# The last eight subtiles of a first attention layer, written in a fixed order beside fourteen output products, with some work given to GpSimd

## The chip, the cores and the metric

The kernel runs on one core of one Trainium2 chip. The metric is the device time of one launch in microseconds (us), as a median over several runs. The engines named below are TensorE (PE in the profile, its weight loads PEld), VectorE (DVE), ScalarE (ACT), GpSimd (POOL) and SyncE (SP, which here only issues transfers).

## The reference

Two cross-attention layers follow each other, all in 32-bit floats. There are 4 batches of 1024 tokens, 1024 wide, and each batch has 64 context rows.

- Layer 0: queries `x @ Wq + bq`, 32 heads of width 32, keys and values of 8 groups made from the context, scores plus a mask, softmax over 64 keys, values, then `x1 = layernorm(out @ Wo + bo + x) * gamma + beta`.
- Layer 1: keys and values of 16 heads of width 64 from the layer-normed context, queries from `x1`, softmax, values, and `y = x1 + tanh(gate) * (out @ Wo1.T)`.

## The kernel before

**Tiles.** The 4096 tokens are 32 subtiles of 128 tokens, 16 pairs of 256 and, later, 8 groups of two pairs (`NQUAD`). Eight subtiles are a block (`SUB`, `NBLK` = 4).

**Seven products for eight.** Big products are made by a Strassen-Winograd scheme: a left matrix in four blocks (A11, A12, A21 stored as S3, A22) and a right one (B11, B12 stored as T1, B22, B21) give sums S1 to S4 and T1, T2, T3, N4, and seven block products, each four 128x128 by 128x512 steps (eight matmul records) into a PSUM bank. Some banks, called X and V, stay open over several products. VectorE adds a bank into the result rows.

**Layer 0.** The queries of a block are made first (`query_steps`, L532) and stored in DRAM. `mix(t, count)` (L727) then attends to subtile t while it pulls `count` steps from the generator `other_work` (L887), which for blocks 1 to 3 makes the next block's queries. Attention of one subtile is made of two halves of 16 heads (`attend0`, L610):

- `front(c)`: scores of one half by TensorE into a two-bank PSUM tile "big" (L636), and a VectorE pass that adds the mask and writes the half to SBUF (L640). The queries of a subtile come by a 512 KB load (L603).
- `largest(e)`: VectorE maximum (L647), then VectorE subtracts it (L650). `alone` keeps some heads out of this: ScalarE then takes the exponential of these head by head with the maximum as bias (L654). For the last eight subtiles it is 4 heads of the first half.
- `exps` on ScalarE (L662), `total(e)`: VectorE sum (L667) and reciprocal (L668), `divide(e)`: VectorE product (L671). Each of these VectorE passes covers 128x1024 numbers.
- `flip(c)`: eight TensorE transposes (L408) and a ScalarE copy to SBUF (for the last eight subtiles two copies of a bank each, L411); `values`: 16 small matmuls (L715), ScalarE copies (L399, or L401 in one piece) and a store of the subtile's output to DRAM (L721).

**The last eight subtiles** (24 to 31, L951 to 955) have no next block to prepare. They run beside 32 steps of `folded_queries` (L848), which multiply layer 1's query weight by its keys: four matmuls each (eight records, L858), two ScalarE copies (L864), and after every second step a 1 MB store issued by GpSimd (`ad<-a`, L870); the weights of four steps come in one 512 KB load (`turned_chunk`, L843). Eight of the 32 steps go ahead of subtile 24 (`FOLD_AHEAD`). The four sums of the right factor Wo (`right_sums`, L188) and the sums of the left factor of pair 0 (`left_out`, L425) are VectorE's. The products of pair 0 (`products`, L449) follow the folded steps (L459): four within subtile 31's `mix`, two around the last flips, one after.

**The order up to here** is a scheduler's: it places the recorded instructions on each engine. From L1047 on (`manual_schedule`) they stand as written. There a small planner takes over: `job(at, end, ...)` puts VectorE, ScalarE, GpSimd and SP work into time slots beside a list of TensorE steps, with due times; it fixes an order, and the hardware still waits by semaphores.

**From L1047 on.** Pair 1's products run as phase ("o", 0) by the list `PAIR`, with four steps F. F is `fold` (L1428): four matmuls (eight records) of layer 1's values and output weight, two ScalarE copies, two 512 KB stores. Then come groups 1 to 7, phases ("o", k), each with two pairs P and Q, by the lists `FOLD_FIRST` (k = 1) and `FOLD`, with three F each for k = 1 to 4, and `MIX` afterwards. In these, joint products a, b, c of both pairs take the place of separate ones; GpSimd makes their sums (L1150, L1154, L1542) and adds the bias `bo` to rows (L990). `close_row` (L1461) normalizes a finished row tile and stores it as `x1`. Layer 1 follows.

**Room.** The pool `weights` has seven 8 KB tiles of the tag "wb": the folded results, the weight chunks, the first rows. `foldpool` has one tile for both kT and vT. `wx` are four single PSUM banks, `big` two double ones. SP issues all loads in order; a load whose room is not free holds those behind it.

## Time and profile before

| what | value |
|---|---|
| median of 3 runs | 1864.75 us (1863.9 to 1869.64) |
| the profiled execution's own time | 1861.73 us |
| its span, first to last instruction | 1859.5 us |
| mean granted TensorE clock | 0.992 of full |
| DRAM to SBUF and back | 355.03 MB, 190 GB/s over the span |
| values of subtile 22 done, on TensorE | 584.6 us |
| scores of subtile 24 start | 593.0 us |
| first product of pair 0 / of pair 1 / of group 1 | 683.3 / 716.4 / 748.8 us |

The stage that the change touches lies from about 585 to 749 us, followed by groups 1 to 4 up to about 961 us. In a timeline line of the profile the first number is the start, the second the time from the first instruction's start to the last one's end, then engine, line, operation, tiles and count; the brackets give the idle time ahead of it and what ended it. A line of a table by stretches gives each engine's busy time in that stretch, with the number of instructions, then the granted clock, the share of the transfer engines that was busy (it can pass 1 a little) and the bytes moved per second.

### The profile page before, as it was taken

How to read it: one execution, taken by the hardware profiler on the slowest of the kernel's cores; microseconds unless marked ns; L12 is line 12 of the kernel's file. 1: busy time of each engine (PE TensorE's matmuls, PEld its weight loads, DVE VectorE, ACT ScalarE, POOL GpSimd, SP SyncE). 2: the span in 40 equal slices, each digit the busy share in tenths (PEclk: the TensorE clock that was granted, in tenths of full speed). 3: DMA queues.
4: the chain of work that ended last, by engine and by line, in shares of the span. 5: the costliest groups of instructions: out<-in, count | busy, mean ns of one | idle time of the engine just before them, and what ended most of it. 6: DMA issues, size and time to landing. Idle time of an engine off the chain costs nothing.

```text
span 1859.5 us, 22201 instructions
## 1 busy us (share of the span) xinstructions
PE 1809.2 (97%) x6856; PEld 1025.0 (55%) x6856; DVE 1368.5 (74%) x1800; ACT 745.0 (40%) x2960; POOL 736.9 (40%) x726
## 2 busy tenths in 40 slices
PE   8999999999999889999999999999999999999998
PEld 7744444444445654455556545656655665566555
DVE  3525589789879995566677887887779777977773
ACT  1111475675635763333322221571607160716150
POOL 0006011111100102833434427658556755675563
PEclk9999999999999899999999999999999999999999
DMA  8996499998786985744567454564378338833741
GB/s 282 182 224 195 131 257 269 258 266 246 225 241 210 324 298 201 270 159 153 181 210 203 147 137 101 165 175 136 114 193 215 113 114 195 213 114 114 181 158 69
DMA packets 228597, 355.03 MB, mean 191 GB/s; under 512 B 29568, under 2 KB 150784, under 8 KB 225280
## 3 DMA queue, kind: packets, MB, share of 16 engines
q1 hardware_dynamic: 175376, 259.23, 49.6%
q0 software_dynamic: 15216, 60.83, 10.8%
q10 hardware_dynamic: 37888, 33.56, 6.1%
q8 instruction: 55, 0.90, 0.2%
q14 instruction: 62, 0.51, 0.1%
HBM read 209.63 MB, written 143.92 MB: 190 GB/s over the span
## 4 chain that ended last, share of the span: by engine, by line
PE 70%; DMA 12%; DVE 10%; ACT 4%; issue 3%; POOL 1%; SPq 1%; DVEq 0%; ACTq 0%; POOLq 0%
PE wx L1085 29%; PE joint L1162 19%; PE wx L532 11%; PE big L636 2%; DMA b_B<-bd 2%; PE wx L380 2%; PE big L380 1%; DMA xq<-in_x_dram 1%; PE big L1438 1%; ACT s L654 1%; DVE s L640 1%; PE big L715 1%; DVE s L671 1%; DMA a_B<-ad 1%; DMA q<-qTd 1%
## 5 line engine op out<-in xcount | busy, mean ns | idle before, releaser
L1296 ACT ACTIVATE s<-s,mx 128x64 f32<-128x64 f32 x512 | 169.9, 334 | 387.3 <-DVE mx L1294 376.5
L654 ACT ACTIVATE s<-s,mx 128x64 f32<-128x64 f32 x488 | 162.7, 336 | 77.1 <-DVE mx L647 74.0
L1096 DVE TENSOR_TENSOR r<-wx,r 128x512 f32<-128x512 f32 x133 | 88.8, 684 | 88.2 <-PE wx L1085 79.5
L990 POOL TENSOR_TENSOR r<-r,bo 128x512 f32<-128x512 f32 x60 | 82.6, 1401 | 147.6 <-DMA r<-in_x_dram 112.3
L532 PE MATMUL wx<-xT,wq_S 128*128 128x512 f32 x256 | 116.6, 599 | 0.8 <-ACT z L543 0.8
L532 PE MATMUL wx<-xB,wq_A 128*128 128x512 f32 x256 | 113.8, 595 | 0.0
L1306 ACT ACTIVATE s<-s,sm 128x64 f32<-128x64 f32 x448 | 108.4, 334 | 12.8 <-DVE sm L1304 12.8
L695 POOL DMA_DIRECT2D pq<-p x76 | 41.5, 553 | 165.1 <-DVE pT L420 66.3
L1469 ACT ACTIVATE junk<-r 128x1024 uint8<-128x1024 f32 x32 | 33.8, 1056 | 167.2 <-DVE r L1176 143.4
L636 PEld LDWEIGHTS big<-kv,q 64*128 64x128 f32 x1024 | 70.0, 193 | 49.4 <-issue 45.3
L640 DVE TENSOR_TENSOR s<-big,m 128x1024 f32<-128x1024 f32 x64 | 77.5, 1216 | 25.0 <-PE big L636 23.6
L1296 ACT ACTIVATION_READ_ACCUMULATOR s<-s,mx 128x1 f32 x512 | 95.9, 187 | 0.0
L814 POOL DMA_DIRECT2D wq1T<-wq1c x64 | 34.9, 552 | 149.3 <-DVE wq1c L420 147.3
L654 ACT ACTIVATION_READ_ACCUMULATOR s<-s,mx 128x1 f32 x488 | 91.9, 188 | 0.0
L1172 DVE TENSOR_TENSOR r<-joint,r 128x256 f32<-128x256 f32 x126 | 52.8, 421 | 41.4 <-PE joint L1162 40.1
L636 PE MATMUL big<-kv,q 64*128 64x128 f32 x1024 | 81.6, 290 | 1.4 <-DMA q<-qTd 1.4
L1176 DVE TENSOR_TENSOR r<-joint,r 128x512 f32<-128x512 f32 x84 | 57.4, 687 | 33.9 <-PE joint L1162 33.7
L532 PEld LDWEIGHTS wx<-xB,wq_A 128*128 128x128 f32 x256 | 48.2, 190 | 58.6 <-issue 57.1
L532 PEld LDWEIGHTS wx<-xT,wq_S 128*128 128x128 f32 x256 | 47.5, 190 | 58.8 <-issue 55.0
L671 DVE TENSOR_TENSOR s<-s,sm 128x1024 f32<-128x1024 f32 x64 | 77.1, 1216 | 1.0
L647 DVE TENSOR_REDUCE mx<-s 128x16 f32<-128x1024 f32 x64 | 75.2, 1212 | 0.9
L870 POOL DMA_DIRECT2D ad<-a x16 | 12.1, 753 | 149.4 <-ACT a L864 149.4
(331 smaller groups left out, 4364.3 us busy)
## 6 DMA issues: line engine op xcount, KB each, us to landing
p<-s POOLq DMA_DIRECT2D x19, 1024.0 KB, 7.7
pq<-p POOLq DMA_DIRECT2D x76, 256.0 KB, 5.9
xq<-in_x_dram SPq DMA_DIRECT2D x64, 256.0 KB, 9.9
q<-qTd SPq DMA_DIRECT2D x32, 512.0 KB, 7.5
oTd<-oT ACTq DMA_DIRECT2D x32, 512.0 KB, 7.2
ad<-a POOLq DMA_DIRECT2D x16, 1024.0 KB, 9.3
r<-in_x_dram SPq DMA_DIRECT2D x32, 512.0 KB, 5.6
bd<-b ACTq DMA_DIRECT2D x32, 512.0 KB, 7.9
```

Source lines behind the costliest of these rows:

```text
L532: nc.tensor.matmul(bank, w_q[a][:, k, sub_ap(i)], rows[b][:, k, :], start=first and k == 0, stop=last and k == HK - 1, skip_group_check=True,)
L636: nc.tensor.matmul(ps[:, at : at + P], q[on, c * 4 + g, :], k0bd[on, b, c, :], start=True, stop=True,)
L640: nc.vector.tensor_tensor(quarters[:, :, c * 8 : (c + 1) * 8], ps.rearrange("p (k a l) -> p a k l", a=NQ, l=Q), mask.rearrange("p e (h l) ...
L647: nc.vector.tensor_reduce(mx[:, e], heads[:, e], AX.XY, ALU.max, negate=True)
L654: nc.scalar.activation(heads[:, e, k], heads[:, e, k], AF.Exp, bias=mx[:, e, k : k + 1], accum_out=sm[:, e, k : k + 1],)
L671: nc.vector.tensor_tensor(heads[:, e], heads[:, e], wide(sm[:, e]), ALU.mult)
L990: on.tensor_tensor(columns(row, h), columns(row, h), bo_sb[h], ALU.add)
L1085: nc.tensor.matmul(banks[key, i], left_at(left[i][s], k), w[m][:, k, :], start=first and k == 0, stop=last and k == HK - 1, skip_group_che ...
L1096: nc.vector.tensor_tensor(at, bank, at, ALU.add)
L1162: nc.tensor.matmul(ps[key], block(a)[:, k, :], (rb | sums[j] if sums else rb)[b][:, k, :], start=first and k == 0, stop=last and k == 1, s ...
L1296: nc.scalar.activation(v[:, h], v[:, h], AF.Exp, bias=mx[:, h : h + 1], accum_out=sm[:, h : h + 1])
L1306: nc.scalar.activation(v[:, h], v[:, h], AF.Copy, scale=sm[:, h : h + 1])
```

## The change

- Subtiles 24 to 31 are no longer given to the scheduler. `manual_schedule` opens ahead of them, and the new `last_mix` writes their order by hand, with a table `PLAN`: for each subtile the number of folded steps, the number of products, and a piece of work (load a pair, make its left sums, add a bias).
- The products of both first pairs are made by `products`: 11 inside the eight subtiles, one after the last folded step, one between the last flips and values, one behind them. The phase ("o", 0) with its list `PAIR` is gone. Its four F go elsewhere: two to the head of `FOLD_FIRST`, and one more to each `FOLD`.
- GpSimd takes the second division of each of the eight subtiles, all four sums of Wo in eight halves (`split_sums`), the left sums of pair 1, and the bias of the first four row tiles (`add_bias_early`, with a bias tile of its own).
- For these subtiles ScalarE copies a double bank at once (L415, L401), and no head has its exponential alone.
- Loads: the four blocks of Wo are asked for ahead of the folded steps, the rows and outputs of pair 0 in subtile 24 and of pair 1 in subtile 27; vT, two chunks of Wo1 and half of group 1's left factor after the last folded step. Six weight chunks and the bias have a pool of three tiles of their own.
- The row tiles 0 to 3 are closed in group 1, and group 1's rows and joint sums get other due times.

```diff
         order = [
             ("X", "A11", "B11", True, False, 0, 0),
+            ("W", "A12", "B21", True, True, 0, 0),
             ("X", "S2", "T2", False, False, 1, 0),
...
-            ("W", "A12", "B21", True, True, 0, 0),
         ]
...
-        alone = BY_HEAD if by_turning(t) else (4, 0) if t >= NSUB - SUB else (0, 0)
+        alone = BY_HEAD if by_turning(t) else (0, 0)
...
         def divide(e):
-            nc.vector.tensor_tensor(heads[:, e], heads[:, e], wide(sm[:, e]), ALU.mult)
+            on = nc.gpsimd if e and t >= NSUB - SUB else nc.vector
+            on.tensor_tensor(heads[:, e], heads[:, e], wide(sm[:, e]), ALU.mult)
...
-            turn(s[:, c * 1024 : (c + 1) * 1024], pT, t >= NSUB - SUB)
+            turn(s[:, c * 1024 : (c + 1) * 1024], pT)
...
+            whole = by_turning(t) or t >= NSUB - SUB - 1
+            ps = big() if whole else [wx(), wx()]
...
+    def split_sums(r):
+        return [
+            lambda o=o, x=x, y=y, k=k: nc.gpsimd.tensor_tensor(r[o][:, k], r[x][:, k], r[y][:, k], ALU.subtract)
+            for o, x, y in (("T1", "T1", "B11"), ("T2", "B22", "T1"), ("T3", "T2", "B11"), ("N4", "B21", "T2"))
+            for k in (slice(0, 2), slice(2, 4))
+        ]
...
+        bias.append(turnedpool.tile([P, H], F32, tag="wq", name="bias_0"))
+        wT, ahead = turned_chunk(0), []
+        nc.sync.dma_start(out=bias[0], in_=bo0.partition_broadcast(P))
         w_o, w_o_loads = right_loads(wo0, "wa", "wo0", "heads")
+        run(w_o_loads)
...
+            for n, step in enumerate(folded_queries(kT, wT, k)):
                 step()
+                for _ in range({11: 1, 12: 1, 14: 2}.get(4 * k + n, 4 * k + n > 14 and len(sums) > 0)):
+                    sums.pop(0)()
                 yield
...
+        vT = foldpool.tile([P, KC, B * S], F32, tag="kvT", name="vT")
+        nc.sync.dma_start(out=vT, in_=vTd)
+        for k in range(2):
+            chunks[k] = chunk(wo1, k, "wo1")
...
+    def last_mix(t, folds, n, then):
+        front, largest, exps, total, divide = attend0(t)
+        front(0)
+        front(1)
+        if t + 1 < NSUB:
+            load_queries(t + 1)
+        next(work)
+        then()
+        largest(0)
+        exps[0]()
+        if n:
+            ready.pop(0)()
+        if t - 2 in turned:
+            turned.pop(t - 2)[1]()
+        turned[t - 1][0](0)
+        largest(1)
+        exps[1]()
+        next(work)
+        total(0)
+        divide(0)
+        turned[t - 1][0](1)
+        total(1)
+        divide(1)
+        for _ in range(2, folds):
+            next(work)
+        turned[t] = outputs0(t)
+        if n > 1:
+            ready.pop(0)()
...
+    PLAN = (
+        (5, 0, first_pair), (2, 2, first_left), (3, 1, lambda: None), (2, 2, second_pair),
+        (3, 1, lambda: None), (2, 2, second_left), (3, 1, lambda: None), (4, 2, lambda: add_bias_early(first_pair_rows[1])),
+    )
+    for i, (folds, n, then) in enumerate(PLAN):
+        last_mix(last + i, folds, n, then)
+        if makes:
+            makes.pop()()
+    next(work)
+    ready.pop(0)()
+    turned.pop(NSUB - 2)[1]()
     flip, values = turned.pop(NSUB - 1)
-    first.pop(0)()
     flip(0)
     flip(1)
-    first.pop(0)()
+    ready.pop(0)()
     values()
...
-    FOLD_FIRST = ("P1 P7 F P6 " + LEAVES).split()
-    FOLD = ("P1 | P6 | P7 F " + LEAVES).split()
-    PAIR = "P1 P7 F P6 P2 F P5 P4 F P3 F".split()
+    FOLD_FIRST = (
+        "F F P1 Q1 P6 F P7 P5 cS1 cS2 cS3 cS4 aS1 aS2 F Q7 c2 c1 Q6 c6 aS3 a2 c7 aS4 Q5 " + END
+    ).split()
+    FOLD = ("P1 | P6 | F P7 F " + LEAVES).split()
...
-    go(phase(("o", 0), [ahead_a], w_o, [second_rows], joint=False), PAIR)
+    bo_sb = both_halves(bo0, "bo")
     for i in range(2):
-        turn("o", 1, i, 3.0 * i, 12.0, (28.0, 44.0)[i], lands=8.0, room=lambda: True)
+        turn("o", 1, i, -1.0, 4.0 + 12.0 * i, (6.0, 22.0)[i], lands=6.0 + 10.0 * i, room=lambda: True)
+    output_rows(1, -1.0, 28.0)
```

## The prediction

> **What bounds the kernel now.** I read the page first, then the stage by stretches, then the timelines of TensorE and VectorE, the chain of waits and the transfers.
>
> ```profile
> span 1859.5 us, 22201 instructions
> ...
> PE 1809.2 (97%) x6856; PEld 1025.0 (55%) x6856; DVE 1368.5 (74%) x1800; ACT 745.0 (40%) x2960; POOL 736.9 (40%) x726
> ```
>
> TensorE sets the end: 97% busy. But the share is an average, and busy is a modelled figure. By stretches of 20 us, the last eight subtiles stand out:
>
> ```profile
> 600.00:620.00 20.00, 15.52 (x113) 10.87 (x112) 15.41 (x17) 15.73 (x38) 1.51 (x2) 0.83 1.05 362
> 620.00:640.00 20.00, 17.44 (x166) 13.03 (x164) 19.38 (x22) 15.49 (x41) 3.01 (x4) 1.00 0.91 293
> 640.00:660.00 20.00, 18.19 (x162) 13.29 (x162) 19.27 (x27) 15.15 (x33) 1.51 (x2) 0.91 1.06 362
> 660.00:680.00 20.00, 14.65 (x118) 11.41 (x118) 17.71 (x18) 14.73 (x38) 2.26 (x3) 0.91 0.88 298
> ```
>
> TensorE (first busy figure) has gaps and a lowered clock, VectorE (third) is full, GpSimd (fifth) nearly empty, the transfer engines (last two) saturated in two of the four. After 720 us TensorE is at 20 of 20 in most stretches, so only this stage can give much. VectorE's period, from one subtile's scores to the next's:
>
> ```profile
> 622.89 2.35 DVE L640 TENSOR_TENSOR s<-big,m 128x1024 f32<-128x1024 f32 x2
> 625.27 2.35 DVE L647 TENSOR_REDUCE mx<-s 128x16 f32<-128x1024 f32 x2
> 627.54 2.08 DVE L650 TENSOR_TENSOR s<-s,mx 128x768 f32<-128x768 f32 x2
> 630.17 2.16 DVE L667 TENSOR_REDUCE sm<-s 128x12 f32<-128x768 f32 x2 [0.55 <-ACT s L662]
> 632.25 0.37 DVE L668 RECIPROCAL sm<-sm 128x16 f32<-128x16 f32 x2
> 632.54 2.35 DVE L671 TENSOR_TENSOR s<-s,sm 128x1024 f32<-128x1024 f32 x2
> 634.81 2.35 DVE L640 TENSOR_TENSOR s<-big,m 128x1024 f32<-128x1024 f32 x2
> ```
>
> It is 11.9 us, nearly all work. TensorE's work beside it is less, and after each gap of some 2 us it runs slowly:
>
> ```profile
> 603.21 2.81 PE L715 MATMUL wx<-pT,kv 64*32 64x512 f32 x16 [2.05 <-ACT pT L415]
> 607.39 2.08 PE L636 MATMUL big<-kv,q 64*128 64x128 f32 x16 [1.36 <-DMA q<-qTd]
> 609.23 1.94 PE L858 MATMUL wx<-kT,wq1T 64*128 64x256 f32 x8
> 610.93 1.13 PE L636 MATMUL big<-kv,q 64*128 64x128 f32 x16
> ```
>
> The same 16 score matmuls take 2.08 us and, 3.5 us later, 1.13.
>
> **How much is there.** From 584.6 (values of subtile 22 done) to 748.8 (first product of group 1) are 164.2 us. TensorE's work in it, from dense rows: 32 folded steps at 1.03 (61 records in 7.82 us, eight a step) 33.0; 16 score halves at 1.05, 16.8; nine pairs of flips at 1.97, 17.7; nine values at 1.05, 9.5; 14 products at 3.44 (starts 716.38 and 719.82) 48.2; four F at 1.92 (starts 723.34 and 725.26) 7.7. Sum 132.9, so 31.3 us are gaps and slow running. The change keeps all this work and moves the four F behind the first product of group 1 or into groups 1 to 4, where TensorE has no gap to hide them: they cost 7.7 there as here. So compare one point, T, the end of the 14th product: before it is 748.8 - 7.7 = 741.1, and it can't be below 584.6 + 125.2 = 709.8. Gain = 741.1 - T, plus what changes in group 1.
>
> **The new cycle.** VectorE a subtile: four times 2.35 (scores, maxima, subtraction, sums, now all of 1024), one division 1.18, reciprocals 0.37: 10.9. Dropping `alone` adds 0.46 of that (2.08 and 2.16 become 2.35) and takes four head-by-head exponentials (1.35 from 614.61 to 615.96) off ScalarE. A product's addition is 0.69.
> - Subtile with one product, three folded steps: VectorE's first addition stands between the two subtractions and waits for scores 1.05, folded step 1.03, product 3.44, 0.2 latency: 5.7 after the period's start. After it 0.6, then maximum, subtraction, sums, division (five passes of 1.18) and reciprocals 0.4: 12.6. TensorE's work, 2.1 + 3.1 + 3.44 + 1.05 + 1.97 = 11.7, lies inside.
> - Two products, two steps: TensorE 2.1 + 2.06 + 6.88 + 1.05 + 1.97 = 14.1, VectorE inside.
> - Subtile 25 also has pair 0's left sums on VectorE, 2.7 (653.61 to 656.3): 12.6 + 0.6 + 2.7 = 15.9.
>
> Subtile 24's scores still wait for their query load (VectorE idles 1.01 ahead of 594.46), so three right sums of 2.28, 2.23 and 2.28 taken from VectorE at 581 to 593 give nothing by themselves. Start of 24: 594.5; of 25: 605.4; then 15.9, 12.6, 14.1, 12.6, 14.1, 12.6 to subtile 31 at 687.3; its TensorE work with four steps, 16.1 less the 1.05 already done; then three products, two values, one pair of flips, 14.4. T = 716.8, if nothing is late.
>
> **What can be late.**
> - *Transfers.* The second load of the burst at subtile 24 took 18 us:
>
> ```profile
> 589.12 18.14 DMA q<-qTd
> ```
>
> It competes with four 1 MB stores issued from 588.7 to 594.6. The change queues 1 MB more ahead of subtile 25's queries on SP (bias, one chunk earlier) and 2 MB (rows and outputs of pair 0) behind them, ahead of subtile 25's first product. At the 410 GB/s seen there 1 MB is 2.6 us: queries at about 610 to 611 instead of 607.3, when VectorE could start at 605.4: 6 late. Pair 0's 2 MB need 5.1 more and share with stores: 617 to 619, when TensorE wants them at 614: 4 late, and the product then starts at a lowered clock. Bounds 0 (burst over sooner) and 14; I take 10. From subtile 26 on a subtile moves some 2.6 MB in 13 us, 200 GB/s, and there is slack.
> - *GpSimd's passes.* No row shows its division of 128x1024. Nearest are its 128x512 sums, 1.28 alone and 1.83 crowded: 2.5 to 3.7. It starts when VectorE goes on to the next scores and is wanted 8 us into the next period: nothing, unless GpSimd is held by a store's wait. Taking the division off VectorE is in the 10.9.
> - *VectorE beside GpSimd.* In group 1 the two disturb each other:
>
> ```profile
> 754.23 1.28 POOL L1542 TENSOR_TENSOR sums_a<-wo_B 128x512 f32<-128x512 f32 x1
> 759.61 1.71 POOL L1542 TENSOR_TENSOR sums_a<-sums_a,wo_B 128x512 f32<-128x512 f32 x1
> ```
> ```profile
> 760.12 3.42 DVE L1490 SCALAR_TENSOR_TENSOR r<-r,norm,beta 128x512 f32<-128x512 f32 x2
> 804.50 1.41 DVE L1490 SCALAR_TENSOR_TENSOR r<-r,norm,beta 128x512 f32<-128x512 f32 x2
> ```
>
> Alone 1.28 and 0.70 (1.41 for two), side by side 1.71 each. So a VectorE pass of 1024 with two SBUF inputs (subtraction, division) may lose 2.0 beside GpSimd. The eight halves of Wo's sums lie in subtiles 24 to 27, three such passes each: bounds 0 and 9 x 2.0 = 18. By the written order the sums meet one subtraction in subtile 26 and little in 25, where VectorE waits for loads: I take 2.
> - *Start of group 1.* SP's second bias load of the planner reuses room of the last output store; before it stood 23 us for that (issue 694.76 to 717.7) and came 3.5 after the store's issue. After, the store is issued 1.9 ahead of T, so the load comes at T + 1.6, behind it the row tile (median landing 5.6) and two GpSimd bias passes: ready at T + 11. The third product of group 1 needs sums that stand behind that addition on VectorE: it starts at T + 13 instead of T + 10.8 (F F 3.9, two products 6.9). Group 1 before loses 2.81 at 764.26 and 2.0 by a product of 5.40 after it; I set one against the other: 0, bounds -5 and +5.
> - *A fourth F a group* needs a free "wb" tile; ScalarE waited 7.3 for such stores in all before. Bounds 0 and 4, I take 0.
> - Whole-bank copies: 0.99 for two of 0.58, off the path: 0, either way.
>
> **The sum.** T = 716.8 + 10 + 2 = 728.8; gain 741.1 - 728.8 = 12.3. The profiled execution is 1861.7 (span 1859.5 and 2.2 around it): 1849.4. It lies 3.0 below the median of the three runs, so 1852.4 for a median: 1852.
>
> *A rule that speaks against the change.* The Trainium skill, "SBUF — State Buffer", section "SBUF: two separate sides", says that a VectorE pass with two SBUF inputs and a GpSimd pass that reads SBUF exclude each other for a whole instruction. The rows above agree in kind (1.71 is about one pass behind the other, not a small tax). Taken at its worst, each of the nine passes waits out a GpSimd half of 2.6, some 23 us (an estimate from that page and the 1.28 row), and the gain would be gone.
>
> **The rivals.**
> 1. *Loads on time.* For it: from subtile 26 there is slack, and the burst's length is seen once only. Against: 408 to 414 GB/s from 596 to 608. T = 718.8, gain 22: 1842.
> 2. *TensorE closes up.* Waits overlap, VectorE's addition costs less than reckoned; T comes within 4 of its floor, 709.8, group 1 loses its stall: gain 30, 1835.
> 3. *Nothing to speak of.* The load burst at its upper bound 14 and the collisions at 6 to 8: gain 12.3 - 4 - 5 = 3: 1861. This also holds the case that the fixed order only moves the gaps.
> 4. *Slower.* Group 1's start, starved of loads: vT shares one tile with kT, so its load waits for the last folded step, and SP holds all of group 1's loads behind it; 7 MB then stand in one queue from about T - 17. If the first biased row is ready not at T + 11 but past T + 29, as when it lands as late as the 18 us load and the bias waits behind it, the stall eats the 12.3 and 5.6 more; at T + 35 the time is 1864.8 + 10 = 1875. Against: transfers are light there (some 60 to 260 GB/s before), and the needed row is seventh or so in the queue.
>
> **How the numbers follow.** Forecast (gain 6 to 18) 0.43; rival 1 0.26; rival 2 0.07; rival 3 0.13; rival 4 0.11. A measurement of this kernel can tell about 0.3%, 5.6 us, from no change: faster 0.76, same 0.13, slower 0.11. The range leaves out the lowest of rival 2 and most of rival 4 and takes in the bounds of loads and collisions: 1835 to 1866.
>
> **What would show it.** Right: subtile periods (L640) of about 12.6 and 14.1 in turn from 26 on; GpSimd's first division beginning as the next scores' pass does; a first gap ahead of subtile 25's scores or its first product, ended by a load of q or o; the 14th product ending near 729; four F in each of groups 1 to 4, TensorE without gaps there. Wrong: no such gap (rival 1); periods of 15 us and more, with VectorE's L650 or L672 stretched to over 2 us (collisions); a long stop ahead of group 1's third product, ended by a load or a bias (rival 4). A mistake in the cycle itself would show as TensorE idle in the two-product subtiles.

## The result, and the profile after

The changed kernel takes **1889.70 us** (median of 4 runs, 1889.32 to 1897.76), the kernel before 1864.33 (4 runs, 1862.05 to 1869.64): a ratio of 1.0142, with the interval 1.0108 to 1.0177. It is slower by some 25 us, where 12 were to be gained. The profiled execution took 1889.41 us; its span is 28.1 us longer than before's.

The head of the page of the changed kernel:

```profile
span 1887.6 us, 22128 instructions
...
PE 1813.6 (96%) x6856; PEld 1020.2 (54%) x6856; DVE 1379.3 (73%) x1777; ACT 734.9 (39%) x2871; POOL 789.2 (42%) x753
```

TensorE's busy time is 4 us more, the span 28: the rest is idle. VectorE has fewer instructions than before and more busy time, so some of them got longer. The stage in stretches of 20 us (columns as before: TensorE, its weight loads, VectorE, ScalarE, GpSimd, clock, share of the transfers, GB/s):

```profile
600.00:620.00 20.00, 11.58 (x73) 8.31 (x72) 10.94 (x7) 6.18 (x12) 13.33 (x8) 0.72 1.05 404
620.00:640.00 20.00, 20.00 (x131) 10.49 (x132) 17.26 (x21) 7.00 (x9) 6.85 (x5) 0.94 0.47 143
...
680.00:700.00 20.00, 15.00 (x94) 8.99 (x94) 19.79 (x14) 6.26 (x8) 13.68 (x13) 0.85 0.46 149
...
800.00:820.00 20.00, 18.16 (x72) 12.96 (x70) 14.74 (x22) 5.39 (x11) 19.86 (x16) 1.00 0.40 155
```

Two things differ from before. In the first line everything waits: TensorE 11.6, VectorE 10.9, with the transfers full. In the line from 680, VectorE is "busy" for 19.79 us with 14 instructions, of which none takes more than 1.23 alone (17 together at most); that is where GpSimd, too, is busiest in the stage. Behind the stage, at 800, GpSimd is full.

Where nothing disturbs it, the cycle is as forecast. The timeline of subtile 28 on VectorE:

```profile
665.27 2.36 DVE L640 TENSOR_TENSOR s<-big,m 128x1024 f32<-128x1024 f32 x2 [0.20 <-issue]
...
668.91 1.22 DVE L650 TENSOR_TENSOR s<-s,mx 128x1024 f32<-128x1024 f32 x1
...
677.91 2.36 DVE L640 TENSOR_TENSOR s<-big,m 128x1024 f32<-128x1024 f32 x2
```

The period is 12.64 us (12.6 was forecast), the subtraction 1.22. One subtile later, in the timeline of VectorE and GpSimd:

```profile
680.65 0.80 POOL L873 DMA_DIRECT2D ad<-a  x1 [0.82 <-ACT a L867]
681.47 2.42 POOL L435 TENSOR_TENSOR S<-o 128x256 f32<-128x256 f32 x2
681.55 1.75 DVE L650 TENSOR_TENSOR s<-s,mx 128x1024 f32<-128x1024 f32 x1
683.86 1.41 POOL L435 TENSOR_TENSOR S<-S,o 128x256 f32<-128x256 f32 x2
685.09 8.75 DVE L650 TENSOR_TENSOR s<-s,mx 128x1024 f32<-128x1024 f32 x1
685.23 1.26 POOL L443 TENSOR_TENSOR o<-o 128x512 f32<-128x512 f32 x1
686.46 1.40 POOL L435 TENSOR_TENSOR S<-o,S 128x256 f32<-128x256 f32 x2
687.83 4.92 POOL L973 TENSOR_TENSOR r<-r,bias 128x512 f32<-128x512 f32 x4
```

The second subtraction starts at 685.09 and ends at 693.84, 1.09 us after GpSimd's last pass (692.75). VectorE does not lose one pass of GpSimd; it waits out the whole run and then does its own work. Such a wait is called a lock below. Five subtractions of the stage end like that: 6.05 at 615.17, 3.03 at 638.73, 3.43 at 654.01, 8.75 at 685.09 and 5.10 at 715.41 (with the 1.75 of 681.55, an excess of 20.8 us over 1.22 each). Each ends 1.09 us after the end of a run of GpSimd passes, and in front of each of the five runs stands a store issued by GpSimd, like the one at 680.65. The three long ones (6.05, 8.75 and 5.10) wait for two, eight and four passes; those of 3.03 and 3.43 begin when a single pass of 2.3 us is left, so they would also fit a wait for one pass. How a lock reaches TensorE, in the timeline of ScalarE and TensorE at the place just shown:

```profile
693.88 1.06 ACT L662 ACTIVATE s<-s 128x1024 f32<-128x1024 f32 x1 [6.92 <-DVE s L650]
695.79 1.01 ACT L415 COPY pT<-big 128x1024 f32<-128x1024 f32 x1
696.86 2.08 PE L636 MATMUL big<-kv,q 64*128 64x128 f32 x16 [5.00 <-ACT pT L415]
```

ScalarE's exponentials wait 6.92 us for the subtraction, the copy behind them is late, and TensorE waits 5.00 for the bank that the copy frees. The load burst is there too, on TensorE:

```profile
608.76 3.66 PE L636 MATMUL big<-kv,q 64*128 64x128 f32 x32 [4.45 <-DMA q<-qTd]
616.98 6.36 PE L461 MATMUL wx<-wo_B,o 128*128 128x512 f32 x8 [3.70 <-DMA o<-oTd]
764.64 5.40 PE L1163 MATMUL wx<-wo_T,S_o 128*128 128x512 f32 x8 [4.09 <-DVE S_o L1113]
```

Subtile 25's queries stop it for 4.45, pair 0's outputs for 3.70, and the product after the second gap runs slowly (6.36 for some 3.6). The third line is group 1's third product.

**Where the 28 us are.** Compare T, the end of the 14th product (before 741.1, forecast 728.8, after 749.0), and the first products of the groups behind it. All four F of pair 1 have moved, so their number in each stretch has to be taken into account.

| stretch | before | after | difference with equal F |
|---|---|---|---|
| up to T | 741.1 | 749.0 | +7.9 |
| T to group 2's start | 61.5 with 7 F | 65.2 with 4 F | +3.7 and 3 F (5.8): +9.5 |
| groups 2 to 4 | 158.3 with 9 F | 172.5 with 12 F | +14.2 less 3 F (5.8): +8.4 |
| the rest | | | +2.3 |

T is counted from an execution's first instruction, and the executions are not equally far when the stage begins: the values of subtile 22 are done at 584.6 in the profile of the kernel before, at 581.2 in the change's. From there to T it is 156.5 before and 167.8 after, 11.3 us more; the prediction's sum gave 144.2 (728.8 - 584.6).

The stage's periods, from one subtile's scores to the next's, are 20.4, 23.6, 15.3, 14.9, 12.6, 20.6 and 13.3, then 37.2 to T; without lateness 10.9, 15.9, 12.6, 14.1, 12.6, 14.1, 12.6 and 29.5 were reckoned. The long ones are 24 (loads), 25 (loads and a lock together), 29 and the end.

### The profile page after: what moved, and what is told of

Same layout as the page of the kernel before. It is cut to its first block, busy times and chain, and to the rows that moved or that the text cites. A ratio compares the mean times of both kernels' runs of the same rounds, so it can differ in the third digit from the quotient of the medians.

```text
span 1887.6 us, 22128 instructions
## 1 busy us (share of the span) xinstructions
PE 1813.6 (96%) x6856; PEld 1020.2 (54%) x6856; DVE 1379.3 (73%) x1777; ACT 734.9 (39%) x2871; POOL 789.2 (42%) x753
## 4 chain that ended last, share of the span: by engine, by line
PE 65%; DVE 12%; DMA 11%; ACT 5%; issue 4%; POOL 1%; SPq 1%; ACTq 0%; DVEq 0%; POOLq 0%
PE wx L1163 24%; PE joint L1240 17%; PE wx L532 13%; PE big L636 2%; PE wx L461 2%; DMA b_B<-bd 2%; PE wx L380 1%; PE big L380 1%; DMA x<-r 1%; ACT s L654 1%; DVE s L650 1%; DVE s L640 1%; DMA p<-s 1%; DMA r<-in_x_dram 1%; PE big L717 1%
## 5 line engine op out<-in xcount | busy, mean ns | idle before, releaser
L1374 ACT ACTIVATE s<-s,mx 128x64 f32<-128x64 f32 x512 | 169.9, 333 | 389.2 <-DVE mx L1372 378.2
L654 ACT ACTIVATE s<-s,mx 128x64 f32<-128x64 f32 x456 | 151.9, 336 | 68.2 <-DVE mx L647 65.3
L1174 DVE TENSOR_TENSOR r<-wx,r 128x512 f32<-128x512 f32 x126 | 83.8, 684 | 79.4 <-PE wx L1163 61.8
L1374 ACT ACTIVATION_READ_ACCUMULATOR s<-s,mx 128x1 f32 x512 | 95.6, 187 | 0.0
L654 ACT ACTIVATION_READ_ACCUMULATOR s<-s,mx 128x1 f32 x456 | 85.8, 188 | 0.0
L1176 DVE TENSOR_TENSOR s<-wx,key_bias 128x512 f32<-128x512 f32 x64 | 42.9, 683 | 37.3 <-PE wx L1163 25.3
L672 DVE TENSOR_TENSOR s<-s,sm 128x1024 f32<-128x1024 f32 x56 | 67.9, 1217 | 1.2
```

The lines of the kernel that those rows point to most:

```text
L654: nc.scalar.activation(heads[:, e, k], heads[:, e, k], AF.Exp, bias=mx[:, e, k : k + 1], accum_out=sm[:, e, k : k + 1],)
L672: on.tensor_tensor(heads[:, e], heads[:, e], wide(sm[:, e]), ALU.mult)
L1174: nc.vector.tensor_tensor(at, bank, at, ALU.add)
L1374: nc.scalar.activation(v[:, h], v[:, h], AF.Exp, bias=mx[:, h : h + 1], accum_out=sm[:, h : h + 1])
```

## The experiments

The theory after reading the two traces: the stage is lost to VectorE's subtractions that wait for runs of GpSimd passes, and behind T the work that stood beside pair 1's products now crowds groups 1 to 4. The rivals: the load burst alone makes the stage late; or group 1 is starved by its loads (rival 4 of the prediction). Each run below is the changed kernel with one edit, unless told otherwise. T and the groups are from the one profiled execution, in us. "Stage" is from the end of subtile 22's values to T: that end lies between 580.5 and 585.6 in these executions, so "stage" compares better than T. "P to P" is from group 1's first product to group 2's, with 2 F in the change, 3 before and in spread_folds, 5 in calm_front and calm_all; "2 to 4" is the sum of these groups, with 12 F in the change and 9 in three_folds, calm, calm_front, calm_all and spread_folds.

| run | median (range) | ratio to before (95%) | T | stage | P to P | 2 to 4 | group 5 |
|---|---|---|---|---|---|---|---|
| before | 1864.33 | 1 | 741.1 | 156.5 | 53.8 (3 F) | 158.3 (9 F) | 46.0 |
| the change | 1889.70 (1889.32–1897.76) | 1.0108–1.0177 | 749.0 | 167.8 | 60.8 | 172.5 | 46.0 |
| left_bias_moved | 1889.58 (1886.66–1896.21) | 1.0106–1.0162 | 745.2 | 163.0 | 63.3 | 174.1 | 46.4 |
| wo_sums_vector | 1895.97 (1894.18–1900.05) | 1.0139–1.0181 | 751.8 | 167.8 | 63.2 | 174.3 | 46.0 |
| bo_by_gpsimd | 1887.38 (1882.40–1889.48) | 1.0091–1.0136 | 748.3 | 167.3 | 57.3 | 175.0 | 46.0 |
| three_folds | 1896.29 (1891.63–1898.52) | 1.0159–1.0200 | 750.0 | 167.8 | 61.3 | 161.3 | 64.4 |
| bias_behind | 1890.05 (1887.44–1896.55) | 1.0130–1.0179 | 749.2 | 167.9 | 61.0 | 168.7 | 46.0 |
| later_products | 1902.51 (1900.59–1903.94) | 1.0200–1.0231 | 761.8 | 177.3 | 63.0 | 170.2 | 46.4 |
| calm | 1880.56 (1877.95–1885.17) | 1.0078–1.0125 | 742.6 | 160.5 | 55.5 | 159.3 | 61.4 |
| calm_front | 1883.54 (1881.12–1887.55) | 1.0082–1.0121 | 742.1 | 160.7 | 72.8 | 162.0 | 46.0 |
| lighter_burst | 1892.20 (1888.52–1895.09) | 1.0127–1.0161 | 748.9 | 166.6 | 63.6 | 174.6 | 46.0 |
| calm_all | 1873.11 (1871.08–1874.19) | 1.0027–1.0056 | 731.8 | 148.7 | 73.3 | 160.0 | 46.5 |
| stores_by_scalar | 1878.50 (1876.87–1883.41) | 1.0054–1.0101 | 735.9 | 154.4 | 61.3 | 171.0 | 46.0 |
| division_vector | 1897.23 (1892.70–1898.72) | 1.0138–1.0193 | 755.6 | 170.0 | 63.5 | 172.4 | 46.2 |
| all_four_folds | 1865.80 (1860.01–1874.40) | 0.9992–1.0024 | 729.2 | 148.7 | 55.3 | 172.5 | 46.0 |
| all_scalar_stores | 1868.53 (1861.60–1872.77) | 1.0004–1.0037 | 734.6 | 153.0 | 58.6 | 169.3 | 46.6 |
| spread_folds | 1872.36 (1869.88–1876.33) | 1.0032–1.0063 | 731.8 | 148.8 | 57.7 | 161.6 | 56.5 |

They are told in the order in which they ran.

### First: who is in VectorE's way

**left_bias_moved.** Pair 1's left sums go back to VectorE, the early bias behind the subtiles.

```diff
-        products_of(second_pair_rows, "0_1", nc.gpsimd)
-        makes.pop()()
-        add_bias_early(second_pair_rows[1])
+        products_of(second_pair_rows, "0_1", nc.vector)
...
+    add_bias_early(first_rows)
+    add_bias_early(second_rows)
     next(work)
```

> Edit to the changed kernel: pair 1's left sums go from GpSimd to VectorE, at the end of subtile 29, and the bias of the first four row tiles is added by GpSimd behind its last division instead of in subtiles 29 and 31. Theory 1 (VectorE's subtraction stands still as long as GpSimd has passes in a row): the subtraction of 8.75 us in subtile 29 and that of 5.10 in subtile 31 become 1.2 each; VectorE gets 2.7 of sums; the period of subtile 29 falls from 20.6 to about 14, the 14th product ends near 740 instead of 749.0, and the whole is 7 to 10 us shorter, about 1881. Rival (the long subtraction only covers what TensorE or a load would lose anyway): periods stay within 2 us, the time within 3 us of 1890.

The long subtractions of subtiles 29 and 31 are gone, so GpSimd's run is their cause. But T came only 3.8 earlier, to 745.2, not to about 740, and the stage is 4.8 shorter: VectorE's own sums cost 2.7 in period 29, TensorE had new gaps in period 30 (1.58 and 1.33), and the late bias held a product's addition at the end (a gap of 2.12). Groups 1 to 4 then gave it back (63.3 for 60.8 and 174.1 for 172.5), and the median did not move. The cause is right, the size of the gain was not.

**wo_sums_vector.** The four sums of Wo return to VectorE, two of them in subtile 24.

```diff
-        sums = split_sums(w_o)
+        sums = right_sums(w_o)
```

> Edit to the changed kernel: the four sums of Wo go from eight GpSimd passes in subtiles 24 to 27 to four VectorE passes, two ahead of subtile 24's scores and two behind its last sum, where VectorE stands idle for 7.7 and 9.0 us. Theory 1: the subtractions of 6.05, 3.03 and 3.43 us in subtiles 25, 26 and 27 become 1.2. Since subtile 25's first product waits for its load until 617 and ends at 623.4 whatever VectorE does, the first of these gives nothing, the other two 2 to 3 us: about 1887. Rival (the 6.05 us subtraction is what makes subtile 25 late): 6 to 8 us, about 1882. If instead the sums push subtile 24 back, the time rises by up to 4.

The long subtractions of 25 to 27 are gone. Yet subtile 26 still starts 25.0 behind 25 (612.94 to 637.89; 23.6 in the change), because the first product waits 5.55 for its load, to 620.72: the 6.05 lay beside a wait for data and cost little by itself. Two other runs say the same: in bo_by_gpsimd and three_folds, whose stage is the change's, this subtraction began just ahead of GpSimd's run and took 1.2, and subtile 25's period was 25.0 and 25.2 all the same. Subtile 29's first subtraction became one of 11.23, where the two had been 1.75 and 8.75. The stage is as long as the change's (167.8); T is later only because this execution was 2.8 later when the stage began. The median is 6.3 higher; of that the trace shows 4.2 in groups 1 to 4, and why they are longer is open.

**bo_by_gpsimd.** The planner's bias load goes to GpSimd's queue, so that SP's is free.

```diff
-    bo_sb = both_halves(bo0, "bo")
+    bo_sb = both_halves(bo0, "bo", nc.gpsimd)
```

> Edit to the changed kernel: the load of the planner's bias, for which SyncE stands still from 732.4 to 750.5 until the last output store has left, is issued by GpSimd, which is idle then; SyncE can go on to group 1's remaining left factor and rows. Theory (the held queue makes group 1's start late): the first row lands before 750 instead of 761.6, VectorE's first addition no longer waits 11.8 us for it, TensorE's gap of 4.09 at 760.6 and the slow product of 5.40 behind it go, and the whole is 5 to 7 us shorter, about 1884. Rival (the room of these rows is itself taken as long, or the biased row is late for GpSimd's sake): the gap stays within 1 us and the time within 2 us of 1890.

In the changed kernel SP stands on this load from 732.39 to 750.5, because its room comes from the last output store. The group 1 lines of the changed kernel's timeline:

```profile
732.39 18.15 SPq L1055 DMA_DIRECT2D bo<-in_bo_dram  x2
...
761.63 0.69 DVE L1174 TENSOR_TENSOR r<-wx,r 128x512 f32<-128x512 f32 x1 [11.82 <-DMA r<-in_x_dram]
```

The rows come behind it and land 12.6 after T. With the edit the gap of 4.09 and the slow product behind it are gone and P to P falls by 3.4; groups 2 to 4 give 2.5 back. The median falls by 2.3, where 5 to 7 were expected. So rival 4's mechanism exists, for 3.4 us and not for 28.

**lock_probe** leaves the whole computation out and lets VectorE and GpSimd passes run against each other.

> A kernel that leaves the whole computation out and only times VectorE and GpSimd passes side by side; its output is mostly a copy of x. GpSimd runs of eight 128x512 subtractions, 1.27 us each alone, beside VectorE passes that start 0.7 us later. Theory 1 (starvation): one 128x1024 subtraction of two SBUF inputs takes about 1.2 plus all that is left of GpSimd's run, 9 to 10 us in all. Rival (exclusion for one instruction at a time): it waits out one GpSimd pass, 1.2 + 1.3 = at most 2.5 us, and three in a row alternate with GpSimd's passes. VectorE passes with one SBUF input (maxima) or with a PSUM input keep 1.2 us in both. If nothing is stretched, the 8.75 us in the changed kernel have another cause.

Alone, a VectorE pass of 128x1024 with two SBUF inputs takes 1.22 and a GpSimd pass of 128x512 1.26. Side by side they take turns: 2.10 to 2.17 and 2.24. Maxima (one input) and a pass with an input in PSUM are not touched (1.21, 1.22). No pass waited out a run, so the mechanism that I had named, starvation by back-to-back passes alone, is not it.

### Second: behind the stage

**three_folds.** Three F a group instead of four; the freed ones fall to group 5.

```diff
-    FOLD = ("P1 | P6 | F P7 F " + LEAVES).split()
+    FOLD = ("P1 | P6 | P7 F " + LEAVES).split()
```

> Edit to the changed kernel: three F instead of four in each of groups 2 to 4, as before; the three left over go to group 5. Nothing ahead of group 2 is touched. From group 2's first product to that of group 5 the changed kernel takes 172.5 us, the kernel before 158.3; 5.8 of the difference are three F, 8.4 are gaps of TensorE that end with GpSimd's sums lS or VectorE's additions. Theory (the fourth F of a group pushes row closings, row loads and with them GpSimd's bias in front of lS): the stretch takes about 158 to 160, and with 5.8 of F in group 5 the whole is 6 to 8 us shorter than 1889.6, about 1882. Rival (these groups are late because group 1 hands them its lateness): the stretch still takes 165 or more after the 5.8 are taken off, the time stays within 3 us.

Groups 2 to 4 fall from 172.5 to 161.3: 5.8 for three F, and 5.4 of gaps that the fourth F had brought. But group 5 with three F takes 64.4, where 46.0 and 5.8 make 51.8. Its timeline:

```profile
1006.29 2.12 ACT L1519 ACTIVATE b<-big,tanh_gate 128x1024 f32<-128x1024 f32 x2 [9.04 <-DMA bd<-b]
1007.46 3.78 PE L1516 MATMUL big<-wo,vT 64*128 64x512 f32 x8 [5.38 <-ACT b L1519]
```

ScalarE waits 9.04 for a store to free its output tile, TensorE 5.38 for ScalarE, and the next F runs slowly (3.78 for 1.99). The time rose by 6.6 us, where a fall of 6 to 8 was expected. F has a price by its place.

**bias_behind.** GpSimd's bias passes get later due times in groups 3 to 5, so that joint sums come first.

```diff
-                return now + 9.0
+                return now + (14.0 if 2 < k < 6 else 9.0)
```

> Edit to the changed kernel: the planner's guess of how long a row load of groups 3 to 5 takes goes from 9 to 14 us, so that GpSimd's bias of one row, which waits about 10 us for that load, stands behind the last two of the four sums lS instead of in front of them. Four F a group stay. Theory of the order (lS behind a bias that waits for a load is what holds TensorE): the stops for lS in groups 3 and 4 (1.9, 1.3 and 0.2 us, each with some slow running after it) go, 3 to 5 us shorter, about 1885. Rival (the rows themselves are late because of the fourth F, whatever the order): the gaps move to VectorE's additions of group 4 and 5, time within 2 us of 1889.6.

Groups 2 to 4 take 168.7 instead of 172.5: in the changed kernel GpSimd stood still for a row's load (9.63 before a bias pass at 917.05) with joint sums behind it that TensorE then waited for. The order is worth 3.8 in the trace. The profiled execution was 2.0 faster, the median the same: smaller than this measurement tells.

**later_products.** Subtile 24 without loads of pair 0, everything one subtile later.

```diff
-        (5, 0, first_pair), (2, 2, first_left), (3, 1, lambda: None), (2, 2, second_pair),
+        (4, 0, lambda: None), (5, 0, first_pair), (2, 2, first_left), (2, 2, second_pair),
```

> Edit to the changed kernel: the first products move from subtile 25 to subtile 26, pair 0's loads from subtile 24 to 25, and each later subtile takes a product more instead (folded steps 4, 5, 2, 2, 3, 2, 3, 3). Theory (subtiles 24 and 25 are held by a burst of transfers: scores at 611.5 instead of 605.4, the first product at 617 for its load and 6.4 us long): subtile 25 runs without the wait for pair 0's outputs, its period falls from 23.6 to 15 or less; the product it gives up costs 3.4 later; the 14th product ends 3 to 6 us earlier, at about 744, and the time is near 1886. Rival (the burst only moves on): subtile 25's scores still start at 611, and subtile 26 waits for pair 0's outputs instead: no gain or a loss of up to 4.

Slower by 13, more than either the theory or its rival had said. Subtile 25's scores still came only at 616.7, two subtractions became 10.21 and 9.92 long, and T went to 761.8, with a stage of 177.3.

**calm** joins four edits: pair 1's sums on VectorE and the bias late, `bo` by GpSimd, three F.

> Four edits to the changed kernel together: pair 1's left sums by VectorE; the early bias by GpSimd behind its last division, pair 1's rows first; the planner's bias loaded by GpSimd; three F a group. If each of the losses stands by itself, their sum goes: 4 to 6 in the stage, 3 in group 1, 6 to 8 in groups 2 to 4: about 1873 to 1876. If groups 1 to 5 are held by a chain that does not run through TensorE's stage (rows, closings, GpSimd's sums), what is won in the stage is lost again in group 1, as in the run that moved left sums and bias: 1880 or more.

T falls by 6.4 to 742.6 (the stage by 7.3), P to P to 55.5, groups 2 to 4 to 159.3 (158.3 before), and group 5 takes 61.4, near the 64.4 of three_folds. The median falls by 9 us, to 1880.6, where 1873 to 1876 stood for losses that add up. In the trace those ahead of group 5 do add up; the 9.6 that group 5 takes beyond its three F is more than what is missing.

### Third: the burst, and why the lock is kept

**calm_front** is calm with the F of group 5 in group 1 (seven there).

```diff
-        "F F P1 Q1 P6 F P7 P5 cS1 cS2 cS3 cS4 aS1 aS2 F Q7 c2 c1 Q6 c6 aS3 a2 c7 aS4 Q5 " + END
+        "F F P1 Q1 F F P6 F P7 P5 F cS1 cS2 cS3 cS4 aS1 aS2 F Q7 c2 c1 Q6 c6 aS3 a2 c7 aS4 Q5 " + END
```

> The kernel with four edits (left sums of pair 1 by VectorE, early bias behind the last division, the planner's bias loaded by GpSimd, three F a group) with the three F that had gone to group 5 put into group 1 instead, two of them behind its first two products. There group 5 took 61.4 us, 9.6 more than 46.0 and three F. Theory (F suits a group as long as its output tile and weights come free in time; group 1 has gaps that F can fill): group 5 is back at 46, group 1 grows from 55.5 by 4 to 6, groups 2 to 4 stay near 159: 1880.6 less 9 to 11, about 1871. Rival (F's outputs wait for room wherever the fourth and further F stand): group 1 grows by 12 or more and the time stays at 1878 to 1882.

Group 5 is back at 46.0, but P to P is 72.8: TensorE waited 3.92 and 4.46 for ScalarE's output of F and 4.84 for GpSimd's joint sums. The gain of the one is the loss of the other, and about 1871 was missed by 12.

**lighter_burst.** The bias load moves out of subtile 24, and pair 0's outputs are asked for ahead of its rows.

```diff
         r = wpool.tile([P, 2, H], F32, tag="wb", name=f"r0_0_{pair}")
-        for u in range(2):
-            nc.sync.dma_start(out=r[:, u], in_=x[sub_ap(2 * pair + u), :])
         o = pool.tile([P, KC, 2 * P], F32, tag=tag, name=f"o2_{pair}")
         nc.sync.dma_start(out=o, in_=oTd[pair])
+        for u in range(2):
+            nc.sync.dma_start(out=r[:, u], in_=x[sub_ap(2 * pair + u), :])
```

> Edit to the changed kernel: the early bias is loaded in subtile 27 instead of ahead of subtile 24, and of a pair's two loads the outputs go ahead of the rows. Theory (bytes queued ahead of what subtile 25 needs make it late): 0.5 MB less is 1.3 us at 410 GB/s and the order of the pair's loads another 2.6: scores of subtile 25 start at about 610 instead of 611.5, its first product at 613 instead of 617; the first addition can still not come before 621 because VectorE's subtraction waits for GpSimd until then, so the 14th product ends 2 to 4 us earlier and the time is 1886 to 1888. Rival (the four and more stores of 1 MB own the transfer engines whatever is asked for behind them): no change within 1.5 us.

Its timeline:

```profile
609.53 2.36 DVE L640 TENSOR_TENSOR s<-big,m 128x1024 f32<-128x1024 f32 x2 [5.90 <-DMA m<-in_mask_dram]
612.85 3.67 PE L461 MATMUL wx<-wo_B,o 128*128 128x512 f32 x8 [1.32 <-DMA o<-oTd]
613.17 6.33 DVE L650 TENSOR_TENSOR s<-s,mx 128x1024 f32<-128x1024 f32 x1
```

The loads come earlier: scores at 609.5 for 611.5, the first product at 612.9 for 617.0, and at full speed. Subtile 26 is not earlier (636.0 for 635.1), and T is 748.9: a subtraction of 6.33 and a left sum of 5.63 take the place of the load. This mirrors wo_sums_vector. Two waits lie side by side in subtile 25, and to take away one of them gains nothing: the median, 1892.2, is no better than the change's.

**calm_all** is calm_front with the lighter burst and the sums of Wo earlier.

```diff
-                for _ in range({11: 1, 12: 1, 14: 2}.get(4 * k + n, 4 * k + n > 14 and len(sums) > 0)):
+                for _ in range({7: 2, 11: 4, 17: 1, 18: 1}.get(4 * k + n, 0)):
```

> All edits together: those of the kernel with seven F in group 1, the lighter burst, and the first six of Wo's eight half sums moved ahead of VectorE's work of subtile 25 (two behind the eighth folded step, four behind the twelfth), where VectorE waits for loads. If the losses add up, it gains over the kernel with seven F in group 1: 4 to 6 by subtile 25's first product starting early and no long subtraction there, 2 by subtile 26: about 1865, level with the kernel before. If sums ahead of subtile 24 hold up its subtraction and the loads stay as late as they are, nothing is gained or 2 to 3 are lost.

T is 731.8 and the median 1873.1, where about 1865 was expected. The longest subtraction is 3.28, and the stage takes 148.7: 19.1 less than the change's and 7.9 less than before's. The time is still 0.4% longer than before's, all of it lost behind T.

**lock_probe2** leaves the whole computation out. Eight parts: eight GpSimd passes with one VectorE pass beside them, with other data, other shapes, readers on ScalarE, and in three parts a 512 KB store issued by GpSimd just ahead of its run.

```diff
+    nc.gpsimd.dma_start(out=y[6 * P : 7 * P, :], in_=z)
     nc.gpsimd.tensor_tensor(g[:, 0:512], c[:, 0:512], d[:, 0:512], ALU.subtract)
     nc.gpsimd.tensor_tensor(g[:, 512:1024], c[:, 512:1024], d[:, 512:1024], ALU.subtract)
...
     nc.vector.tensor_tensor(strided(s), strided(s), wide2(mx), ALU.add)
```

> A second kernel that leaves the computation out and only times passes. In the first, VectorE's subtraction of two SBUF inputs waited out one GpSimd pass of a run (2.1 us for 1.2) and they took turns; in the changed kernel it waited for 2 to 9 passes in a row. Here the passes have the forms of the changed kernel: maxima, then an addition in place to one half of the heads with a broadcast input, beside eight GpSimd passes. Parts: plain; with a transfer issued by GpSimd ahead of its run; with GpSimd's results read by ScalarE; with VectorE's input flat; without the maxima just ahead; both transfer and reads; GpSimd in place on eight tiles; the same behind a transfer. If one of these is what keeps VectorE out until the run ends, the pass takes 8 to 11 us in the parts that have it and about 2.1 in the others; if it is 2.1 in all, the cause of the long waits stays open.

The timeline of its first two parts:

```profile
25.10 2.10 DVE L76 TENSOR_TENSOR s<-s,mx 128x1024 f32<-128x1024 f32 x1
26.08 2.25 POOL L69 TENSOR_TENSOR g<-c,d 128x512 f32<-128x512 f32 x1
...
35.80 0.70 POOL L85 DMA_DIRECT2D out_dram<-z  x1 [0.37 <-issue]
36.52 1.27 POOL L86 TENSOR_TENSOR g<-c,d 128x512 f32<-128x512 f32 x1
36.87 10.53 DVE L95 TENSOR_TENSOR s<-s,mx 128x1024 f32<-128x1024 f32 x1
...
45.06 1.25 POOL L93 TENSOR_TENSOR g<-c,d 128x512 f32<-128x512 f32 x1
```

Without a store, 2.10, and the GpSimd pass beside it is stretched to 2.25: they take turns. With a store ahead, the same VectorE pass takes 10.53 and ends 1.1 after GpSimd's last pass, and the GpSimd passes are not stretched at all. In the eight parts: 2.08 to 2.10 in all five without a store, 10.32 to 10.69 in all three with one.

### Fourth: one word

**stores_by_scalar.** ScalarE issues the 1 MB stores; GpSimd's passes stay as they are.

```diff
             if cc % 2:
                 n = cc // 2
-                nc.gpsimd.dma_start(
+                nc.scalar.dma_start(
```

> Edit to the changed kernel, one word: the sixteen 1 MB stores of the folded results are issued by ScalarE, which has just made their data, instead of GpSimd. GpSimd's passes stay where they are. Theory (a transfer issued by GpSimd right ahead of a run of passes keeps VectorE out until the run ends, as in the second probe): the subtractions of 6.05, 8.75 and 5.10 us in subtiles 25, 29 and 31 become at most 1.2 and one GpSimd pass, 2.5 to 3.6; VectorE and GpSimd take turns; the 14th product ends 6 to 10 us earlier, near 741, and the time falls to 1880 to 1885. Rival (VectorE is kept out whatever stands ahead of the run): the long subtractions stay, and ScalarE's 0.55 us an issue makes the stage 0 to 3 us longer.

11.2 us faster than the change (1876.87 to 1883.41 against 1889.32 and more); T falls by 13.2 to 735.9, more than the 6 to 10 that were expected. The timeline, at the place shown of the changed kernel:

```profile
679.96 1.97 DVE L650 TENSOR_TENSOR s<-s,mx 128x1024 f32<-128x1024 f32 x1
680.80 2.41 POOL L435 TENSOR_TENSOR S<-o,S 128x256 f32<-128x256 f32 x2
683.18 6.93 POOL L973 TENSOR_TENSOR r<-r,bias 128x512 f32<-128x512 f32 x4
683.78 1.75 DVE L650 TENSOR_TENSOR s<-s,mx 128x1024 f32<-128x1024 f32 x1
```

The same GpSimd work lies beside the same subtractions: 1.97 and 1.75 instead of 1.75 and 8.75, and GpSimd's bias is stretched instead (6.93 for 4.92). The longest subtraction of the stage is 2.92. From 26 on the periods are 12.4 to 15.9. The edit also moves the stores in time, and the first product comes 4.9 earlier (612.1) without waiting for its load; but subtile 26's scores start at 635.5, as in the change (635.1), so the whole gain lies behind them, where the change has four of its five locks: from there to T it is 100.3 instead of 113.9. What is left is subtile 25, whose period is 25.1: pair 0's left sums on VectorE take 4.37 and 2.89 by turns with GpSimd's sums of Wo, and the product behind them, after a gap of 3.60, takes 6.75.

**division_vector.** The second division returns to VectorE.

```diff
-            on = nc.gpsimd if e and t >= NSUB - SUB else nc.vector
-            on.tensor_tensor(heads[:, e], heads[:, e], wide(sm[:, e]), ALU.mult)
+            nc.vector.tensor_tensor(heads[:, e], heads[:, e], wide(sm[:, e]), ALU.mult)
```

> Edit to the changed kernel: the second division of each of the last eight subtiles goes back to VectorE. By the prediction VectorE's 1.2 us a subtile is on the path where a subtile has one product or none: 3 to 6 us more in subtiles 26 to 31, about 1894. Rival (TensorE or GpSimd's other passes set these periods): within 2 us of 1889.6. If the division on GpSimd delays something, the time falls.

Slower by 7.5. Of the 6.6 by which T is later, 4.4 were there when the stage began (595.6 for 591.2); the stage itself is 2.2 longer (170.0) and P to P 2.7. One trace with a difference of 2.2 leaves the division's own worth open in size; the sign is as predicted.

**all_four_folds** is the changed kernel with the bias late, the left sums on VectorE, `bo` by GpSimd, the lighter burst, the sums of Wo earlier and bias_behind; four F a group as in the change.

> The kernel with all edits (1873.1), but with four F in each of groups 1 to 4 as in the change and GpSimd's bias of rows behind the last sums lS in groups 2 to 4. There group 1 took 73.3 us with seven F, of which 13 were waits for F's output and GpSimd's sums behind them. Theory (seven F in a group wait for room, four cost 2 to 3 us a group): from the 14th product to the sixth group 277 to 280 us instead of 284.2, in all about 1866 to 1869. Rival (group 1 is held by GpSimd's 55 us of sums and biases whatever F do): no gain.

1865.8 in ten runs, level with before (0.9992 to 1.0024): together these edits take away 24 of the 25 us. T is 729.2, 11.9 earlier than before; 4.1 of that were there when the stage began, and the stage, 148.7, is 7.8 shorter than before's. Behind T, up to group 6, 278.3 us against 265.9: the whole gain is given back there.

**all_scalar_stores** has the same, with ScalarE's stores, and the left sums left on GpSimd.

> As the previous kernel, with the 1 MB stores issued by ScalarE and pair 1's left sums on GpSimd again. Theory (without transfers of its own GpSimd takes turns with VectorE): the left sums cost VectorE at most two GpSimd passes instead of 2.7 us of its own, subtile 29's period falls from 17 to about 15, the subtractions beside Wo's sums stay under 3.6 us: 1 to 4 us faster than the previous kernel, about 1863 to 1867, level with the kernel before. If VectorE is kept out in any case, it is 4 to 8 us slower than the previous kernel.

1868.5, where 1 to 4 less than all_four_folds were expected: a miss. T is 734.6 and the stage 153.0, 4.3 longer than in all_four_folds. Of that, 3.6 come ahead of subtile 24's scores, which start 13.5 behind the values of subtile 22 instead of 9.9 (12.6 in stores_by_scalar); in both of these runs TensorE waits there for the query load, which it doesn't in the others. So the stores on ScalarE's queue have a price of their own, whose reason was not looked into; from subtile 24 on the two kernels are level within 0.7.

**spread_folds** distributes the F: five in group 1, three in 2 to 4, two in group 5; otherwise as all_four_folds without bias_behind.

```diff
-        "F F P1 Q1 P6 F P7 P5 cS1 cS2 cS3 cS4 aS1 aS2 F Q7 c2 c1 Q6 c6 aS3 a2 c7 aS4 Q5 " + END
+        "F F P1 Q1 P6 F P7 F P5 cS1 cS2 cS3 cS4 aS1 aS2 F Q7 c2 c1 Q6 c6 aS3 a2 c7 aS4 Q5 " + END
...
-    FOLD = ("P1 | P6 | F P7 F " + LEAVES).split()
+    FOLD = ("P1 | P6 | P7 F " + LEAVES).split()
+    FOLD_TWO = ("P1 | P6 | P7 " + LEAVES).split()
```

> The kernel with four F in groups 1 to 4 (1865.8) with the F spread otherwise: five in group 1, three in groups 2 to 4, two in group 5; the planner's guess of the row loads is again the original. Theory (a fourth F costs groups 2 to 4 2 to 3 us each beyond its own work, three F cost group 5 9 to 12 for room and transfers): groups 2 to 4 take 159 instead of 172.5, group 5 takes 54 to 57 instead of 46.0, group 1 58 to 60 instead of 55.3; the sum is 2 to 5 us shorter, about 1862. Rival (each place costs the same, the loss is the F's transfers and room): within 2 us of 1865.8.

1872.4, where about 1862 was expected: a miss. Groups 2 to 4 are down to 161.6, but P to P is 57.7 and group 5, with two F, 56.5 (49.9 by its work). These are near what was expected for each, and their sum, 275.8, is 2.0 above the 273.8 of all_four_folds: the expected parts (159, 58 to 60, 54 to 57) did not hold the gain that was read from them. No version beats the kernel before.

## Why the prediction was wrong, step by step

In the profiles, 40.4 us lie between forecast and measurement: 20.2 up to T (728.8 to 749.0), and 9.5, 8.4 and 2.3 behind it. Two steps failed, one on each side of T; a third was too small.

**The step that failed: "VectorE beside GpSimd".** The prediction took 2 us for it, with bounds 0 and 18. Measured were 20.8 us of excess in the subtractions, 16.0 of them in subtiles 26 to 31; the lateness of the periods from 26 to T is 18.4 us, and 13.6 of it goes when GpSimd issues no stores (stores_by_scalar). Two things were wrong in it. It counted Wo's eight halves only, and left out that the change also gives pair 1's left sums and the early bias to GpSimd, which make two of the three longest waits (8.75 and 5.10). And it took for granted that one VectorE pass waits for one GpSimd pass, as the rows of group 1 had shown (1.71 each). The runs show that this holds without a transfer ahead (2.1, lock_probe, lock_probe2), and that behind a transfer issued by GpSimd a VectorE pass waits for the whole run (10.3 to 10.7 for eight passes; in the kernel one word is worth 11.2 us, although GpSimd's passes stay). The prediction's own sign for a collision, an L650 stretched to over 2 us, is what the trace shows.

The Trainium skill, "SBUF — State Buffer", section "SBUF: two separate sides", says that the lock is held for one instruction and that the other engine blocks for that long. The turns of lock_probe agree (2.1 for 1.22); the 10.53 with a store ahead does not, and there the measurement decides. The estimate of 23 us that the prediction had from this page was near the 20.8, but by luck: nine waits for one pass each were reckoned, five waits came, and the 8.75 and 5.10, more than half of the excess, lie behind passes that were not counted. The same section advises to issue transfers from ScalarE or SyncE, because VectorE can keep GpSimd from writing descriptors. The advice would have been right here (11.2 us), for the opposite direction: it was VectorE that waited.

**The second: "Start of group 1: 0, bounds -5 and +5" and "A fourth F a group ... bounds 0 and 4".** Measured were +9.5 and +8.4, outside the bounds. The prediction compared one point, T, and took the rest of the kernel as unchanged. But pair 1's products had been the cover under which row tiles were closed, GpSimd added biases and made group 1's sums, and four F drained their outputs: from 720 to 760 us GpSimd was busy for 22.0 us before and for 6.0 in the change. Of the 9.5, 3.4 were the late bias load and its slow product (bo_by_gpsimd). Of the 8.4, 3.8 were the order on GpSimd (bias_behind) and 5.4 the fourth F (three_folds); they overlap. The other 6.1 of group 1 are open: GpSimd is full there (19.86 of 20 from 800), which no run tested by itself, and with the F placed otherwise the loss moves to group 1 or 5 instead of going away (calm_front, spread_folds).

**The third: transfers.** 10 us were taken, with bounds 0 and 14. Against the sum, subtile 25 starts 6.1 late and its period is 7.7 too long, 13.8 together; as this execution was 3.3 ahead when the stage began, period 24 itself is 9.5 too long, which makes 17.2. Not all of the 7.7 belongs to transfers, since the lock of 6.05 lies beside it. The times held: queries reached TensorE at 608.8 against 610 to 611, pair 0's outputs at 617.0 against 617 to 619. That they lie beside a lock of about the same length, so that neither alone could be won back, was not seen.

**What was right, and what only looks so.** The cycle: 12.64 in a period of one product, 14.1 in one of two where no subtraction is held (subtile 27 in wo_sums_vector). GpSimd's division: 1.90 us, from subtile 28 on begun with the next scores, and no gap of TensorE ends with it. What the whole-bank copies cost was not measured apart: TensorE waits 3.37, 0.78 and 2.45 for one (L401), each time behind exponentials of ScalarE that had themselves waited for a long subtraction (6.99, 4.72 and 6.39). T of 729.2 and 731.8 in all_four_folds and calm_all is close to the 728.8 of the sum by luck: the sum holds 12 us of lateness, so without the waits it says 716.8, and the all_four_folds execution was 4.1 ahead when the stage began. In length, the stage fell from 156.5 to 148.7, by 7.8 where 12.3 were forecast, and it still holds smaller waits (period 25 is 19.6, a subtraction 3.92); behind T the kernel lost that again. Rival 4, the only one on the slower side, had the right sign, and its mechanism exists, but the gap that TensorE had from it was 4.1 us, not 18 and more, and taking the held load away gave 3.4. Its price at T + 35 is also off by its own rule: 24 us after T + 11 less 12.3 make 1876.5, not 1875; and the transfers, which it called light, moved 332 GB/s in the kernel before from 724 to 741 us. Nothing hangs on either.

## What to carry to other kernels

Compare an edit's whole path to the next point where both versions stand alike, not the end of the stage it repairs: work that stood as cover beside removed products has to be priced where it goes. Look at what GpSimd issues ahead of its passes; a transfer from its queue followed by a run of passes can stop VectorE for the length of the run, and another queue for the transfer removed that, here at a price of some 3 us elsewhere. Where a period is late, take away all waits that end in it at once in one experiment, because two that lie side by side each look free when removed alone.

## What was not expected of the hardware

- A VectorE pass with two SBUF inputs beside eight GpSimd passes took 2.1 us, and 10.3 to 10.7 when GpSimd had issued a transfer just ahead of them. One pass in the kernel did get in after a store (1.75 at 681.55, while GpSimd's first sums ran), and in wo_sums_vector the pass at the same place did not (11.23). Why the engine keeps its place after a transfer is open; only that it does was shown.
- GpSimd's division of 128x1024 takes 1.90 us; its sum of two tiles of the same size takes 2.33 (4.65 for two).
- After gaps of 3.6 to 4.1 us TensorE's next product took 5.40 to 6.75 instead of 3.6, so such a wait cost up to nearly twice its length.
